# Counting the first 64 neighbours by scans along the rows, on the vector engine, in place of triangular matmuls on the tensor engine

## The chip, the cores and the metric

The kernel runs on one core of a Trainium2 chip. The core has a tensor engine (PE, whose weight loads stand as PEld), a vector engine (DVE), a scalar engine (ACT), GpSimd (POOL) and a sync engine (SP); each takes its instructions in order. The metric is the device time of one execution in microseconds (us), as the median of several.

## The reference

Four layers of a graph network over 2708 nodes with 512 features, joined by residuals and layer norms. The change lies in layer 0, and layer 1 uses what layer 0 makes of the adjacency matrix.

```python
# layer 0
Ab = A > 0
keep = Ab & (jnp.cumsum(Ab.astype(jnp.int32), axis=1) <= neibor_num)     # the first 64 neighbours of a row
cnt = keep.sum(axis=1, keepdims=True).astype(X.dtype)
nb_sum = keep.astype(X.dtype) @ X
nb_mean = nb_sum / jnp.maximum(cnt, 1.0)
xj = jax.nn.leaky_relu(nb_mean @ W_nb.T + b_nb)
xi = jax.nn.leaky_relu(X @ W_line.T + b_line)
return xi + jnp.where(cnt > 0, xj, jnp.zeros((), X.dtype))
# layer 1, in short
mask = (adj > 0).astype(x.dtype)
agg = mask @ x / jnp.maximum(mask.sum(axis=1, keepdims=True), 1.0)
```

Layers 2 and 3 are attention layers masked by `adj > 0`. Each layer's result is normed together with its input, `layernorm(x + layer(x))`.

## The kernel before

The 2708 rows lie in 22 tiles of 128 (the last has 20). `maskT` holds the whole adjacency matrix turned, in fp8, in SBUF: `maskT[:, j, :]` has neighbours 128j to 128j+127 on the partitions and all rows along the free dimension. Layers 0 and 1 use it as it is, and so do the attention layers, which want it as 0 and 1.

**First stage of layer 0.** The loop runs over the tiles t of rows. PE turns the tile of x (`transposed`, L120), multiplies it by the neighbour weight into PSUM tile `pm0` and by the line weight into `pm1` (`product`, L221: four fp32 matmuls each, which the profile shows as eight). `keep_y` splits `pm0` into a high part `yH` (ACT, L215) and the rest `yL` (DVE, L216). The second product gets its bias, its leaky ReLU and x, and goes to `r0_dram`. `load_mask` fetches a tile of the adjacency matrix (int32, cast to bf16 by the DMA, from POOL's queue), `count` makes it 0 and 1 and counts it on DVE (L240), then works out four columns of numbers from the count; `turn` transposes it on PE (L254) in three groups through the PSUM tiles `acc`, and ACT copies each group into `maskT` (L258). The masks have two buffers. `pe(...)` ties a PE instruction behind the one before it, so that the order is as written; where it isn't used, a scheduler orders the instructions by its own estimates. `tc.issue_after(i)` ties what stands in it behind instruction i on the same engine. At the start, `transpose_weight` turns the two weights (L132, copied by DVE at L133).

**The sums.** The rows are cut in six blocks (`cuts`): the last two tiles first, then five blocks of four tiles. For each block the loop runs over the 22 tiles j of neighbours; I call one pass a step. `kept` counts along j with a matmul by an upper triangle of ones (L311) into the running count `cum`, which another matmul by its complement (L401) brings to the end of tile j before the next; DVE compares the count with 64 and multiplies by the mask (L313), which gives `kT`, with two buffers:

```python
nc.tensor.matmul(cum[:, :w], upper, maskT[:, j, cols], start=(j == 0), stop=True, skip_group_check=True)
kT = st.tile([P, 512], F32R, name="kT", bufs=2)
nc.vector.scalar_tensor_tensor(kT[:, :w], cum[:, :w], KEEP, maskT[:, j, cols], op0=OP.is_le, op1=OP.mult)
```

Two matmuls for each row tile, by `yH` and by `yL`, add into its accumulator (L408: eight in a step of a full block, four in the first block's). At a block's end ACT scales the accumulators by `rkeep` (L418), and the block's `finish` (bias, leaky ReLU, `r0`, layer norm with a power on POOL at L113 and DVE's L114 behind it) runs among the next block's steps. Among them too run `weights1` (eight products of layer 1's weights) and `vectors` (24 pairs of DVE instructions, L388 and L389, for the later layers), which advance at every `next(later, None)`.

**Layer 1.** Its products loop over the tiles as in the first stage; its own sums (L450) read `maskT` through ACT casts (L447).

Of the kernel before, what the change touches and what calls it, by code (L numbers as in the profile page):

```python
# [30 lines left out]
def kernel(  # L31
# [44 lines left out]
    for c, value in ((iso, 0.0), (has, 0.0), (rdeg, 1.0), (rkeep, 1.0)):  # L76
        nc.vector.memset(c, value)
# [4 lines left out]

    maskT = big.tile([P, NT, NT * P], F8, name="maskT")
    nc.gpsimd.memset(maskT[:, NT - 1, :], 0.0)
    nc.gpsimd.memset(maskT[:, :, N:], 0.0)
# [39 lines left out]
    def transpose_weight(pool, psum, dst, src):  # L125

        for ki in range(KD):
            wr = pool.tile([P, D], F32, name="wr", bufs=4)
# [52 lines left out]
    def leaky(dst, u):  # L181
        nc.vector.scalar_tensor_tensor(dst, u, 0.01, u, op0=OP.mult, op1=OP.max)
# [7 lines left out]
    with ExitStack() as phase:  # L190
        yp = phase.enter_context(tc.tile_pool(name="y", bufs=1))

        upper = yp.tile([P, P], BF16, name="upper")
        make_upper_triangular(nc, upper)
        below = yp.tile([P, P], BF16, name="below")
        nc.vector.tensor_scalar(below, upper, -1.0, 1.0, op0=OP.mult, op1=OP.add)
# [16 lines left out]

        def keep_y(t, n, pm):
            nc.scalar.copy(yH[:n, t, :], pm[:n])  # L215
            return nc.vector.tensor_sub(yL[:n, t, :], pm[:n], yH[:n, t, :].bitcast(F32))  # L216
# [6 lines left out]

        def rows_of(src):
            return early(2, NT, lambda t: fetched(src, t, rows(t)))

        with ExitStack() as ph:
            st = ph.enter_context(tc.tile_pool(name="l0a", bufs=2))
            wnT, wlT = weight(), weight2

            def load_mask(t):
                n = rows(t)
                m = st.tile([P, N], BF16, name="m")
                nc.gpsimd.dma_start(m[:n], adj[t * P:t * P + n, :], max_dma_last_dim=N * 2)
                return m

            def count(t, m):
                n = rows(t)
                cnt = sm.tile([P, 1], F32, name="cnt")
                nc.vector.tensor_scalar(m[:n], m[:n], 0.0, None, op0=OP.is_gt, op1=OP.add, accum_out=cnt[:n])  # L240
                one = slice(t, t + 1)
                nc.vector.tensor_scalar(iso[:n, one], cnt[:n], 0.0, None, op0=OP.is_equal)
                nc.vector.tensor_scalar(has[:n, one], cnt[:n], 0.0, None, op0=OP.is_gt)
                nc.vector.tensor_scalar(rkeep[:n, one], cnt[:n], KEEP, 1.0, op0=OP.min, op1=OP.max)
# [993 lines left out]
```

## Time and profile before

| | |
|---|---|
| median of 6 runs | 3102.53 us (3101.47 to 3105.81) |
| the profiled execution | 3102.03 us, of it span 3100.2 us |
| busy share of the span | PE 97%, PEld 53%, DVE 64%, ACT 45%, POOL 7% |
| first stage of layer 0 | 0 to 216 us of the span |
| sums of layer 0 | 216 to 534 us |
| layer 1's products, its sums | 534 to 690 us, 690 to 940 us |
| attention layers and the end | from 940 us on |

A line of the profile's groups has the code line, the engine, the operation, out<-in with the tiles' names, partitions x elements and type, the count, then after the bar the busy time in us and the mean of one in ns, and after the second bar the idle time of the engine just ahead of these instructions with what ended it. A window's line has each engine's busy time with its count of instructions, then the granted clock of PE, the share of the DMA engines and what they moved.

### The profile page before, as it was taken

What the parts mean: (1) busy time and instruction counts of PE and PEld (TensorE: products, weight loads), DVE (VectorE), ACT (ScalarE), POOL (GpSimd) and SP (SyncE); (2) the same over time, 40 slices, a digit from 0 to 9 for tenths busy, and PEclk for the clock granted to TensorE, in tenths of its full rate; (3) what the DMA queues carried; (4) which work ended last, traced back from release to release, by engine and by line L of the source; (5) the groups of instructions that cost most, each with busy time, mean ns of one, the idle gap of its engine ahead of it and who ended that gap; (6) DMA issues with size and microseconds to landing.
All of it is one profiled execution on the core that took longest, in us unless ns stands there. A gap on an engine that the chain in (4) does not pass through costs nothing.

```text
span 3100.2 us, 37155 instructions
## 1 busy us (share of the span) xinstructions
PE 3000.7 (97%) x14888; PEld 1646.6 (53%) x14888; DVE 1988.8 (64%) x2562; ACT 1400.9 (45%) x1575; POOL 224.8 (7%) x352
## 2 busy tenths in 40 slices
PE   8999999999999999999998999999999999999998
PEld 4556666448888333333357333333367455555555
DVE  5662765212333899999987999999964534355342
ACT  2431000112224688888864888899873000000011
POOL 2220010101110000000012000000000000000001
PEclk9999999999999999999999999999999999999999
DMA  6651421322222000110024000010031000000000
GB/s 141 140 125 35 122 65 38 109 65 86 75 73 81 15 29 29 35 54 30 22 86 153 26 29 28 28 38 32 22 101 45 4 14 17 24 15 21 14 21 20
DMA packets 114287, 163.31 MB, mean 53 GB/s; under 512 B 39494, under 2 KB 62311, under 8 KB 114104
## 3 DMA queue, kind: packets, MB, share of 16 engines
q1 hardware_dynamic: 88152, 109.21, 11.6%
q0 software_dynamic: 16064, 47.95, 5.6%
q10 hardware_dynamic: 9888, 3.67, 0.5%
q8 instruction: 119, 1.95, 0.3%
q14 instruction: 64, 0.52, 0.1%
HBM read 130.92 MB, written 44.55 MB: 57 GB/s over the span
## 4 chain that ended last, share of the span: by engine, by line
PE 67%; issue 19%; DVE 10%; DMA 2%; ACT 2%; POOL 0%; SPq 0%; DVEq 0%; POOLq 0%; ACTq 0%
PE pn L869 13%; PE pm L221 10%; PE po L746 9%; PE acc L450 7%; DVE e L610 6%; PE pm L547 6%; PE acc L408 6%; PE pl L844 5%; PE pl L835 5%; PE pd L677 2%; PE ps_tr L120 1%; ACT c L618 1%; DMA rows<-o_dram 1%; PE acc L254 1%; PE pm L401 1%
## 5 line engine op out<-in xcount | busy, mean ns | idle before, releaser
L610 DVE SCALAR_TENSOR_TENSOR e<-v_bc,ucol,maskT 128x1300 f32<-128x1300 f32 (+3 forms) x836 | 1187.3, 1473 | 345.0 <-PE pn L869 317.8
L618 ACT ACTIVATE c<-e,bcol 128x1300 fp8e4<-128x1300 f32 (+1 forms) x704 | 994.0, 1423 | 112.0 <-DVE e L610 60.2
L746 PE MATMUL po<-e,R 128*64 128x512 f32 (+2 forms) x4224 | 947.0, 550 | 47.4 <-DVE e L610 47.2
L746 PEld LDWEIGHTS po<-e,R 128*64 128x64 f32 x4224 | 340.2, 136 | 601.3 <-issue 385.1
L869 PE MATMUL pn<-e,R 128*128 128x512 f32 (+1 forms) x1056 | 413.5, 542 | 0.2 <-ACT R L565 0.2
L869 PEld LDWEIGHTS pn<-e,R 128*128 128x128 f32 x1056 | 191.0, 190 | 199.6 <-issue 195.9
L547 PE MATMUL pm<-w,xT 128*128 128x264 f32 (+3 forms) x1056 | 247.7, 388 | 3.8 <-DVE R L561 3.0
L547 PEld LDWEIGHTS pm<-w,xT 128*128 128x128 f32 (+1 forms) x1056 | 193.0, 188 | 39.7 <-DVE R L561 3.6
L408 PE MATMUL acc<-yH,kT 128*128 128x512 f32 x484 | 214.0, 442 | 0.0
L837 ACT ACTIVATE w<-pl,b 128x256 f32<-128x256 f32 (+1 forms) x88 | 40.9, 465 | 372.9 <-PE pl L835 372.9
L450 PE MATMUL acc<-yH,mf 128*128 128x512 f32 x484 | 192.7, 398 | 0.0
L408 PE MATMUL acc<-yL,kT 128*128 128x512 f32 x484 | 192.1, 397 | 0.0
L450 PE MATMUL acc<-yL,mf 128*128 128x512 f32 x484 | 190.2, 393 | 0.0
L113 POOL TENSOR_TENSOR ln_rs<-ln_rs,half 128x1 f32<-128x1 f32 x88 | 51.5, 585 | 1710.7 <-DVE ln_rs L112 1710.6
L221 PE MATMUL pm<-w,xT 128*128 128x512 f32 (+1 forms) x384 | 173.1, 593 | 2.5 <-ACT xT L122 1.4
L221 PE MATMUL pm<-weight,xT 128*128 128x512 f32 (+1 forms) x352 | 162.3, 604 | 3.6 <-DVE weight L133 2.8
L313 DVE SCALAR_TENSOR_TENSOR kT<-pm,maskT 128x512 fp32r<-128x512 f32 (+1 forms) x132 | 84.7, 642 | 124.5 <-PE pm L311 123.9
L844 PE MATMUL pl<-lin,w 128*128 128x512 f32 (+1 forms) x352 | 157.4, 592 | 0.0
L835 PE MATMUL pl<-lin 128*128 128x256 f32 (+1 forms) x704 | 153.4, 371 | 3.7 <-DVE lin L768 3.7
L835 PEld LDWEIGHTS pl<-lin 128*128 128x128 f32 x704 | 129.1, 190 | 34.4 <-issue 15.8
L447 ACT CAST mf<-maskT 128x1024 fp32r<-128x1024 fp8e4 (+1 forms) x66 | 64.3, 976 | 164.1 <-PE acc L450 154.1
L215 ACT CAST yH<-pm 128x512 fp32r<-128x512 f32 (+1 forms) x44 | 25.7, 585 | 242.8 <-PE pm L221 242.8
(173 smaller groups left out, 2516.5 us busy)
## 6 DMA issues: line engine op xcount, KB each, us to landing
rows<-x_dram SPq DMA_DIRECT2D x63, 256.0 KB
m<-in_adj_dram POOLq DMA_DIRECT2D x21, 677.0 KB, 6.3
v_bc<-v_dram SPq DMA_DIRECT2D x16, 704.0 KB
x_dram<-u POOLq DMA_DIRECT2D x42, 256.0 KB, 2.3
rows<-o_dram SPq DMA_DIRECT2D x42, 256.0 KB
v_bc<-v_dram SPq DMA_DIRECT2D x16, 650.0 KB
o_dram<-o SPq DMA_DIRECT2D x32, 256.0 KB
rows<-in_x_dram SPq DMA_DIRECT2D x21, 256.0 KB
```

The lines of the kernel that those rows point to most:

```text
L221: order(nc.tensor.matmul(pm[:n], xT[:, k, :n], w[:, k, :], start=(k == 0), stop=(k == KD - 1)))
L313: nc.vector.scalar_tensor_tensor(kT[:, :w], cum[:, :w], KEEP, maskT[:, j, cols], op0=OP.is_le, op1=OP.mult)
L408: nc.tensor.matmul(pa[t], kT[:, (t - b[0]) * P:(t - b[0] + 1) * P], y[:, j, :], start=(j == 0 and y is yH), stop=(j == NT - 1 and y is yL))
L447: nc.scalar.copy(mf[:, :g1 - g0, :], maskT[:, g0:g1, t * P:(t + 1) * P])
L450: nc.tensor.matmul(pa, mf[:, j - g0, :], y[:, j, :], start=(j == 0 and y is yH), stop=(j == NT - 1 and y is yL))
L547: nc.tensor.matmul(pm[a][:n, :D // 2 + heads], xT[:, k, :n], w[:, k, a, :D // 2 + heads], start=(k == 0), stop=(k == KD - 1))
L610: nc.vector.scalar_tensor_tensor(e[:, :w], v[:, :w], ucol[:, j, h:h + 1], maskT[:, j, c0:c0 + w], op0=OP.max, op1=OP.mult)
L618: nc.scalar.activation(c[:, :w], e[:, :w], AF.Sigmoid, bias=bcol[:, j, h:h + 1], scale=STEP, saturate=False)
L746: pe(nc.tensor.matmul(po[i][HO * k:HO * k + HO, :c1 - c0], R2[:, j, h * HO:(h + 1) * HO], e[:, c0:c1], start=(j == 0), stop=(j == NT - 1)))
L835: nc.tensor.matmul(pl[:, :w], self.lin1[:, k, f * P:(f + 1) * P], h[:, k, :w], start=(k == 0), stop=(k == KD - 1))
L844: nc.tensor.matmul(pl[:n], gT[:, f, (t - t0) * P:(t - t0) * P + n], self.lin2[:, f, :], start=(f == 0), stop=(f == KF - 1))
L869: nc.tensor.matmul(pn[k][:, :w], R2[:, j, k * P:(k + 1) * P], e[:, :w], start=(j == 0), stop=(j == NT - 1))
```

## The change

The first 64 neighbours are found along each row, before the mask is turned. ACT makes the mask 0 and 1 by a steep sigmoid and counts it in passing (`count`). DVE runs a scan along the row that starts at -64.5, adds 1 at each neighbour and stops at 0.5, and multiplies the mask by it (`place`): a neighbour that is kept becomes negative, one that isn't becomes 0.5, the rest stays 0. The turned mask holds these numbers, and `kept` is a comparison with 0, without PE. In layer 1's products 22 DVE instructions make `maskT` 0 and 1 again. `place` works in two parts a mask in the first stage and in four parts in the sums.

The masks are taken in the order of the blocks (`turns`). 14 of the 22 pass through the first stage, with three buffers, spread over its tiles; every PE instruction there is bound by `pe`. The other eight go through `other_masks` among the steps of the sums, in two places of SBUF (`w` and `spare`), turned through `pm0` and `pm1`; `weights1` and `vectors` follow in the same chain, which now advances at every step, behind that step's `kept` (`issue_after`). The columns `has` and `rkeep` are worked out for each block at its end (`reciprocals`), `iso` and `rdeg` after the last mask. The raw weights of the start lie in `maskT` instead of buffers of their own, and `maskT`'s two memsets come after the first mask loads.

```diff
         def keep_y(t, n, pm):
-            nc.scalar.copy(yH[:n, t, :], pm[:n])
+            highs[t] = nc.scalar.copy(yH[:n, t, :], pm[:n])
             return nc.vector.tensor_sub(yL[:n, t, :], pm[:n], yH[:n, t, :].bitcast(F32))
...
+        HERE = NT - 8
+        cuts = [(b, min(b + 4, NT)) for b in range(0, NT, 4)]
+        cuts = cuts[-1:] + cuts[:-1]
+        turns = [t for b in cuts for t in range(*b)]
...
+        def count(i, m):
+            t, n = turns[i], rows(turns[i])
+            nc.scalar.activation(m[:n], m[:n], AF.Sigmoid, bias=gate[:n], scale=STEP, accum_out=cnts[:n, t:t + 1])
+
+        def place(i, m, places, part, of):
+
+            n = rows(turns[i])
+            c0, c1 = N * part // of, N * (part + 1) // of
+            nc.vector.tensor_tensor_scan(places[:n, :c1 - c0], m[:n, c0:c1], over[:n].to_broadcast([n, c1 - c0]),
+                                         places[:n, c0 - N * (part - 1) // of - 1:][:, :1] if part else -KEEP - 0.5,
+                                         OP.add, OP.min)
+            return nc.vector.tensor_mul(m[:n, c0:c1], m[:n, c0:c1], places[:n, :c1 - c0])
...
             for t in range(NT):
                 n = rows(t)
-                order = pe if t < 3 else as_it_comes
                 if t > 1:
-                    lows[t] = keep_y(t, n, product(xTs(t), n, wnT, 0, order))
+                    lows[t] = keep_y(t, n, product(xTs(t, order=pe), n, wnT, 0, pe))
                 xT = xTs(t)
                 if t + 1 < NT:
-                    xTs(t + 1)
-                for q in range(0 if t == 2 else t - 1, t) if t > 1 else ():
-                    turn(q, ms[q], order)
-                    if q + 2 < NT:
-                        ms[q + 2] = load_mask(q + 2)
-                pm = product(xT, n, wlT, 1, order)
+                    xTs(t + 1, order=pe)
+                while turned < counted - (t + 1 < NT):
+                    for _ in turn(turned, masks(turned), lambda: sums(BF16, (P, G, P)), pe):
+                        pass
+                    turned += 1
+                now = counted < min(HERE, -(-t * HERE // (NT - 4)))
+                if now:
+                    m, places = masks(counted), st.tile([P, N // 2], BF16, name="places", bufs=1)
+                    with tc.issue_after(highs[t].ins):
+                        count(counted, m)
+                    with tc.issue_after(lows[t].ins):
+                        place(counted, m, places, 0, 2)
+                pm = product(xT, n, wlT, 1, pe)
...
+                if now:
+                    with tc.issue_after(low.ins):
+                        place(counted, m, places, 1, 2)
+                    counted += 1
...
-            def kept(cum, b, j):
+            def kept(b, j):
                 cols, w = slice(b[0] * P, b[1] * P), (b[1] - b[0]) * P
-                nc.tensor.matmul(cum[:, :w], upper, maskT[:, j, cols], start=(j == 0), stop=True, skip_group_check=True)
                 kT = st.tile([P, 512], F32R, name="kT", bufs=2)
-                nc.vector.scalar_tensor_tensor(kT[:, :w], cum[:, :w], KEEP, maskT[:, j, cols],
-                                               op0=OP.is_le, op1=OP.mult)
-                return kT
+                made = nc.vector.tensor_scalar(kT[:, :w], maskT[:, j, cols], 0.0, None, op0=OP.is_lt)
+                return kT, made
...
+            def other_masks():
+
+                def room(i):
+                    r = (ahead.tile([P, 2 * KD * (D + 2 * H)], BF16, name="w", tag="w", bufs=1) if i % 2 else
+                         st.tile([P, 2 * KD * D], BF16, name="spare", tag="spare"))
+                    m = r[:, :N]
+                    load_mask(i, m)
+                    return m, r[:, N:N + N // 4 + 1]
+
+                got = {HERE: room(HERE)}
+                for i in range(HERE, NT):
+                    if i + 1 < NT:
+                        got[i + 1] = room(i + 1)
+                    m, places = got.pop(i)
+                    if i == HERE:
+                        for _ in range(5):
+                            yield
+                    count(i, m)
+                    yield
+                    yield
+                    for part in range(4):
+                        place(i, m, places, part, 4)
+                        yield
+                    psum = (ps_mm.tile([P, G, P], BF16, name=f"pm{k % 2}") for k in range(3))
+                    for _ in turn(i, m, lambda: next(psum)):
+                        yield
+                nc.vector.tensor_scalar(iso, cnts, 0.0, None, op0=OP.is_equal)
+                nc.vector.tensor_scalar(rdeg, cnts, 1.0, None, op0=OP.max)
+                nc.vector.reciprocal(rdeg, rdeg)
+
+            def reciprocals(ts_):
+                nc.vector.tensor_scalar(has[:, ts_], cnts[:, ts_], 0.0, None, op0=OP.is_gt)
+                one = rkeep[:, ts_]
+                nc.vector.tensor_scalar(one, cnts[:, ts_], KEEP, 1.0, op0=OP.min, op1=OP.max)
+                nc.vector.reciprocal(one, one)
...
-            todo, later = iter(()), chain(weights1(), vectors())
-            cum, kT = begin(cuts[0])
+            todo, both = iter(()), chain(other_masks(), weights1(), vectors())
+            kT, nxt_made = kept(cuts[0], 0)
...
                     next(todo, None)
-                    if i == 1 and j > 1 or i > 1 and j % 2 or i == 0 and j == 2:
-                        next(later, None)
+                    with tc.issue_after(nxt_made.ins):
+                        next(both, None)
+                with tc.issue_after(nxt_made.ins):
+                    reciprocals(slice(*b))
...
                 keep_y(t, n, product(xT, n, wnb[0], 0))
+                nc.vector.tensor_scalar(maskT[:, t, :], maskT[:, t, :], 0.0, None, op0=OP.not_equal, saturate=False)
                 if t + 1 < NT:
```

## The prediction

> **What bounds the kernel now.** I read the busy time by stage first, then the groups of layer 0, then the chain of waits there. Stretches of the span (columns: busy us of PE, PEld, DVE, ACT, POOL, then the granted clock, DMA share, GB/s):
>
> ```profile
> core 0: us, PE busy (x) PEld busy (x) DVE busy (x) ACT busy (x) POOL busy (x), PEclk, DMA share, GB/s
> 0.00:216.00 216.00, 203.14 (x957) 107.76 (x958) 124.45 (x217) 79.02 (x132) 60.92 (x76) 0.99 0.63 138
> 216.00:534.00 318.00, 314.00 (x1331) 215.04 (x1330) 177.36 (x318) 22.45 (x41) 24.69 (x38) 0.99 0.23 66
> 534.00:690.00 156.00, 155.28 (x424) 71.95 (x423) 41.35 (x69) 25.26 (x46) 15.90 (x29) 1.00 0.26 85
> ```
>
> The change touches these three: layer 0's first stage (0 to 216), its sums (216 to 534), layer 1's products (534 to 690). PE fills all three. Groups of the first two, with mean ns of one, then idle time before them:
>
> ```profile
> L408 PE MATMUL acc<-yH,kT 128*128 128x512 f32 x484 | 214.0, 442 | 0.0
> ...
> L313 DVE SCALAR_TENSOR_TENSOR kT<-pm,maskT 128x512 fp32r<-128x512 f32 x110 | 75.5, 686 | 112.7 <-PE pm L311 112.4
> L240 DVE TENSOR_SCALAR_CACHE_REDUCE m<-m 128x2708 bf16<-128x2708 bf16 x21 | 62.2, 2964 | 9.4 <-DMA m<-in_adj_dram 9.4
> L311 PE MATMUL pm<-maskT,upper 128*128 128x512 fp8e4 x110 | 41.7, 379 | 0.0
> L401 PE MATMUL pm<-maskT,below 128*128 128x512 fp8e4 x105 | 40.6, 387 | 2.1 <-DVE kT L313 2.1
> L254 PE MATMUL acc<-identb,m 128*128 128x128 bf16 x441 | 28.3, 219 | 0.5 <-DVE m L240 0.5
> ```
>
> Matmuls overlap, so these means aren't their cost: in the sums DVE waits for PE (112.7 us), PE for DVE 4.0 us in all. The cost is the pitch, which the chain of waits shows (start, us, what):
>
> ```profile
> 255.02 3.43 PE pm L221 x8
> ...
> 352.77 1.87 PE acc L408 x8
> 355.09 1.87 PE acc L408 x8
> 357.41 1.87 PE acc L408 x8
> ```
>
> One step of the sums is eight matmuls, 1.87 us (0.233 each), but steps start 2.32 us apart: the counting pair L401 and L311 costs 0.45. An x-row product (L221) takes 3.43.
>
> DVE's prices, from its groups:
>
> ```profile
> L388 DVE TENSOR_TENSOR spare<-spare 128x512 f32<-128x512 f32 x24 | 16.4, 683 | 2.9 <-DMA spare<-in_L_gnn_W_dram 1.9 <-DMA spare<-in_L_gnn_Wo_dram 0.8
> ...
> L765 DVE TENSOR_SCALAR spare<-rows 128x512 f32<-128x512 f32 x21 | 8.8, 424 | 21.8 <-DMA rows<-o_dram 21.7
> ```
>
> 512 elements cost 683 ns with two tensors and 424 with one tensor and constants; L240 (2708 in 2964) gives 1.04 ns an element and some 0.15 us fixed. In the timeline, back-to-back DVE instructions of 0.68 start 0.60 apart, so each costs its duration less 0.08.
>
> [...] Estimate: a new `kept` (512 columns) 0.42, a `not_equal` over 2816 columns 1.63.
> [...]
>
> ```profile
> 3.67 2.69 DVE L64 CAST identb<-ident 128x128 bf16<-128x128 f32 x1 [2.37 <-POOL ident masks.py:199]
> ...
> 3.60 2.07 POOL L85 MEMSET maskT<- 128x2376 fp8e4 x1
> ```
>
> A 128-column cast lasted 2.69 us under GpSimd's memset.
>
> **The change part by part.** The sums run from 217.8 to 533.5, 315.7 us; the six cuts take 27.6, 82.1, 52.3, 50.9, 51.3, 51.1 (starts of L408).
>
> *Counting pairs removed.* 110 steps x 0.45 + 22 narrow ones x (1.16-0.93) = **-54.6**. Left on PE: 968 x 0.233 = 225.5; layer 1's eight weight products, 8 x (3.43+0.44) = 31.0. The remaining 4.6 of the 315.7 are waits for `kT`, which also go.
>
> *Eight masks' transposes moved.* 22 start over 1.42 us in the first stage (113.36 to 114.78), so 8 x 1.42 = **-11.4** there and **+11.4** in the sums. PE's sums: 225.5+31.0+11.4 = 267.9.
>
> *DVE in the sums.* Each step has a `kept` of 0.34. Each mask part adds scan 1.49, product 0.43, and 0.1 for waiting on the scan: 2.37 with the `kept`, against 1.87 of PE. `kT` has two buffers, so DVE runs one step ahead at most, and its excess over a stretch, less one step, stops PE. I added up DVE's work between consecutive `kept`s, in the order in which the built kernel queues it, against PE's. Excesses: cut 0 3.4, cut 1 2.4, cut 2 5.2, cut 3 4.9, cut 4 none (PE has three weight products), cut 5 10.7. In cut 5's first nine steps stand the last vectors, four `finish`es and nine `kept`s, 29.9 us against 16.8; `not_equal`s follow. There PE gets layer 1's first products (7.3 us) early, covering 4.4. Together **+22.2**. The same addition on the kernel before gives 311.3 of the 315.7.
>
> *Waits added in the sums*, **+12**, each estimated. `u`'s scaling at a cut's end now waits for `reciprocals` behind a mask part; four accumulators wait for it: 2. The first mask's load starts when the first stage frees its buffer and shares the DMA with another's (6.3 us each alone, some 11 together, then 2.6 of count): its scan stands in front of step 9's `kept` and is 2.5 late. The 1 MB for layer 1's first weight product is asked for after the last mask left that buffer, three steps ahead (5.6 us), for some 8 us of transfer: 2.5. [...] L114 waited 6.2 us here before, and I add 5.
>
> *First stage.* Tiles start 8.83 us apart, of which the turn is 1.42. A tile with a mask gives DVE 2 x 2.94 + 2 x 0.88 + 3 x 0.61 = 9.5 us, one without 1.8. In runs of three or four mask tiles DVE falls 0.6 back per tile and then blocks the next but one product through L216: 4 over three runs. At the start the fourth copy of the second weight queues behind the first scan, which waits for yH, a table load and the count: pm1 starts at 28.8 instead of 27.0, **+1.8**. Mask DMAs issued before the memsets compete with weights: 1. With the turns: -11.4+4+1.8+1 = **-4.6**.
>
> *ACT.* A count is 2.55 us (L618: 1408 columns 1468 ns, 1300 1378), a turn's casts 2.65; with 1.2 of copies 6.4 of 8.83: hidden. In the sums ACT was busy 22 of 318; 8 x 5.2 more hide.
>
> *SP and POOL.* Eight mask loads cross into the sums, where the DMA share was 0.23; they pass r0 and weight loads, and the waits are those above.
>
> *Layer 1.* The other 13 `not_equal`s add 20 us to DVE's 41 of 156. PE waits for DVE only once a whole product behind (3.43), more than two of them: 0.
>
> **Sum.** Sums 267.9+22.2+12 = 302.1 (-13.6), first stage -4.6: **-18.2**. The profiled execution is 3102.03 (span 3100.2 and 1.8 around it), 0.5 under the median 3102.53: 3083.8 against it, **3084** against the median. A measurement of this kernel can tell some 0.2% (6 us) from no change.
>
> **Unknown costs.** Scan: 0.86 (full rate) to 2.2; I take 1.57. At full rate the sums lose 12 more and the first stage 4; at 2.2 the sums gain 20. Product: 0.51 or 0.86; at 0.86 +10 in the sums, +8 in the first stage. `kept`: 0.42 or 0.69. The 12 of waits: 0 to 22.
>
> **The rivals.**
> 1. *DVE keeps up* (0.17): its excess disappears in slack that I don't see. The sums are 268 to 275, the first stage -11: 3050. For it: in the trace DVE's 43 us in 350 to 400 held PE up by 1.5. Against: 2.37 against 1.87 stands in four steps of each mask.
> 2. [...] (0.11): +18, 3102, no change. No trace row excludes it.
> 3. [...] (0.12), slower. Place: `kept` and `not_equal` on DVE. Price: 0.69 and 3.1. The same addition gives the sums 29 more, mainly in cut 5 (nine `not_equal`s at 3.0 beside 1.87): 3113. It decides from a `kept` of about 0.60. [...]
> 4. *The masks come late* (0.08): [...] ACT's count and DVE's queue wait: 22 x some 1.5 = +33, 3117.
>
> **How the numbers follow.** My case has 0.52. Faster takes it nearly whole (0.50), rival 1 (0.17), a third of rival 2 (0.04) and a little of 3 (0.02): 0.73. Same: rest of mine 0.02, 0.04 of rival 2, 0.03 of the others: 0.09. Slower: 0.18. The range runs from rival 1 (3050) to short of rival 3's value (3110).
>
> **What would show it.** In the profile after: L408's steps 1.87 apart where no mask or `finish` is, longer in cut 2, 3 and 5, PE idle there put down to DVE's `kT`; the scan at 1.57 and 3.0, the product at 0.51, `kept` at 0.42. A scan near 0.86 or a `kept` near 0.69 breaks a price; sums under 285 or over 315 us break the addition; a first stage over 218 breaks its slack.

## The result, and the profile after

The kernel after takes 3094.88 us (median of 17 runs, 3091.37 to 3101.13), the kernel before beside it 3102.28 (37 runs): ratio 0.9977, 95% interval 0.9971 to 0.9984, or 7.4 us less. The forecast was 18.2 us less. The profiled execution after took 3093.61 us, of it span 3091.8.

The windows of the kernel after, as the prediction shows them of the kernel before (columns: busy us of PE, PEld, DVE, ACT, POOL, then the granted clock, the DMA share and GB/s):

```profile
0.00:216.00 216.00, 185.26 (x737) 94.36 (x738) 161.06 (x132) 92.70 (x125) 90.25 (x64) 0.97 0.45 105
216.00:534.00 318.00, 293.25 (x1292) 208.71 (x1291) 218.82 (x410) 68.51 (x90) 44.49 (x49) 0.99 0.36 90
534.00:690.00 156.00, 156.00 (x433) 72.84 (x432) 64.03 (x90) 26.16 (x47) 27.34 (x30) 1.00 0.25 84
```

PE fills the first stage no longer: 185 of 216 us for 203 before. POOL went from 61 to 90 us there, although the change gives it fewer loads there and no new instruction: something holds its instructions up. DVE's groups in the first stage, then POOL's addition of x to `u` in the kernel after and, as L292, in the kernel before:

```profile
L245 DVE TENSOR_TENSOR_SCAN places<-m,places,over 128x1354 bf16<-128x1354 bf16 x13 | 39.4, 3031 | 0.0
L245 DVE TENSOR_TENSOR_SCAN places<-m,over 128x1354 bf16<-128x1354 bf16 x13 | 38.7, 2977 | 10.8 <-ACT m L239 10.4
L248 DVE TENSOR_TENSOR m<-m,places 128x1354 bf16<-128x1354 bf16 x26 | 32.1, 1234 | 0.6
```

```profile
L311 POOL TENSOR_TENSOR u<-u,rows 128x512 f32<-128x512 f32 x21 | 63.7, 3035 | 123.3 <-DVE u L179 123.3
L292 POOL TENSOR_TENSOR u<-u,rows 128x512 f32<-128x512 f32 (+1 forms) x22 | 27.9, 1268 | 117.8 <-DVE u L182 117.8
```

The scans have the forecast price (3.0). The products (L248) average 1234 ns where the forecast assumed 860 (its 0.88 is that, with 0.1 of waiting and less 0.08), and POOL's addition 3035 for 1268 before. The timeline of one mask tile puts the two side by side (start, us, what), DVE and then POOL:

```profile
40.01 3.03 DVE L245 TENSOR_TENSOR_SCAN places<-m,places,over 128x1354 bf16<-128x1354 bf16 x1
43.08 1.75 DVE L248 TENSOR_TENSOR m<-m,places 128x1354 bf16<-128x1354 bf16 x1
44.74 0.68 DVE L216 TENSOR_TENSOR yL<-pm,yH 128x512 fp32r<-128x512 f32 x1
```

```profile
40.19 3.91 POOL L311 TENSOR_TENSOR u<-u,rows 128x512 f32<-128x512 f32 x1 [2.33 <-DVE u L179]
```

The second scan starts 0.2 us ahead of the addition; the addition ends 1.06 us after the scan, and the product then ends 0.73 after the addition. In all 14 mask tiles the addition starts 0.2 us behind a scan and lasts 3.91 to 3.93 us; in the seven full tiles without a mask it lasts 1.26 or 1.27. `yL`, which frees PE's `pm0`, stands behind the product. PE's waits in the first stage (in total, times, longest):

```profile
PE pm L221 <- DVE yL L216: 16.3, 9, 2.4
...
PE pm L221 <- DVE weight L130: 5.2, 1, 5.2
```

And PE after three such waits, with a window on each of the first two products:

```profile
66.19 5.29 PE L221 MATMUL pm<-w,xT 128*128 128x512 f32 x8 [2.45 <-DVE yL L216]
104.45 3.67 PE L221 MATMUL pm<-w,xT 128*128 128x512 f32 x8 [2.45 <-DVE yL L216]
143.50 5.37 PE L221 MATMUL pm<-w,xT 128*128 128x512 f32 x8 [2.44 <-DVE yL L216]
```

```profile
66.10:69.40 3.30, 3.21 (x4) 1.51 (x5) 3.05 (x2) 0.22 (x2) 0.22 (x1) 0.50 0.86 207
104.40:108.20 3.80, 3.75 (x11) 1.81 (x12) 3.15 (x2) 3.15 (x7) 0.19 (x1) 1.00 0.86 184
```

After the first idle of 2.45 us the granted clock was 0.50 for a while and the product took 5.29 us; after the second, as long, it took the usual 3.67. Of five waits of 2.2 to 2.5 us in this stage two were followed by such a slow product (5.29 and 5.37), some 3.4 us together.

Later stages hold a surprise. Layer 1's sums, whose instructions the change leaves alone, took 225.7 us before and take 219.3. The chain in a stretch of 30 us, the kernel before and then after:

```profile
799.91 30.10 PE acc L450 x129
```

```profile
799.97 30.15 PE acc L495 x133
```

30.10/129 is 0.2333 us a matmul, 30.15/133 is 0.2267.

So the time by stages, from profiles. "Start" runs from the second product with the first weight to the third, "tiles" from there to the first matmul of the sums. (In the profiles of this document that second product starts between 16.5 and 25.5 us, with the arrival of the first weights; that is left out here.)

| us | start | tiles | layer 0's sums | layer 1's products | layer 1's sums |
|---|---|---|---|---|---|
| before | 19.9 | 181.1 | 315.3 | 162.2 | 225.7 |
| after | 21.3 | 188.4 | 311.2 | 153.5 | 219.3 |
| forecast change | first stage: -4.6 | | -13.6 | 0 | 0 |

The first two of layer 1's products now start inside the sums, as forecast. At the forecast's 7.3 us for the pair the sums proper fell by 11.4 and the products by 1.4. The first stage is 8.7 longer. From layer 1's sums come 6.4 that no step of the forecast had. (Each row of these tables is a single profile. The programs e5, e8, e11 and e15 below have the kernel after's first stage, instruction for instruction; over the five the tiles took 188.4 to 191.9 us, with two to four slow products. A difference of 3 us in that column says little.)

### The profile page after: what moved, and what is told of

The parts are those of the page before. It is cut to its first block, busy times and chain, and to the rows that moved or that the text cites. A ratio compares the mean times of both kernels' runs of the same rounds, so it can differ in the third digit from the quotient of the medians.

```text
span 3091.8 us, 36738 instructions
## 1 busy us (share of the span) xinstructions
PE 2955.0 (96%) x14630; PEld 1629.6 (53%) x14630; DVE 2088.9 (68%) x2589; ACT 1462.1 (47%) x1621; POOL 286.0 (9%) x350
## 3 DMA queue, kind: packets, MB, share of 16 engines
q1 hardware_dynamic: 88152, 109.21, 11.6%
q10 hardware_dynamic: 9888, 3.67, 0.5%
## 4 chain that ended last, share of the span: by engine, by line
PE 61%; issue 20%; DVE 13%; ACT 3%; DMA 2%; POOL 1%; SPq 0%; DVEq 0%; POOLq 0%; ACTq 0%
PE pn L914 13%; PE po L791 9%; PE pm L221 8%; PE acc L495 7%; PE pm L592 7%; DVE e L655 6%; PE pl L889 5%; PE pl L880 5%; PE acc L450 4%; PE pd L722 2%; PE ps_tr L117 1%; DVE places L245 1%; ACT c L663 1%; DVE w L245 1%; DVE spare L245 1%
## 5 line engine op out<-in xcount | busy, mean ns | idle before, releaser
L450 PE MATMUL acc<-yH,kT 128*128 128x512 f32 x484 | 200.3, 415 | 18.7 <-DVE kT L327 12.8
L592 PEld LDWEIGHTS pm<-w,xT 128*128 128x128 f32 (+1 forms) x1056 | 192.2, 187 | 38.9 <-DVE R L606 4.0
L221 PE MATMUL pm<-w,xT 128*128 128x512 f32 (+1 forms) x384 | 177.0, 604 | 17.0 <-DVE yL L216 16.3
L495 PE MATMUL acc<-yH,mf 128*128 128x512 f32 x484 | 188.4, 389 | 0.0
L221 PE MATMUL pm<-weight,xT 128*128 128x512 f32 (+1 forms) x352 | 161.8, 602 | 6.5 <-DVE weight L130 5.2
L722 PE MATMUL pd<-c,parts_c 128*12 128x384 fp8e4 (+2 forms) x2816 | 130.9, 307 | 0.0
L221 PEld LDWEIGHTS pm<-w,xT 128*128 128x128 f32 (+1 forms) x384 | 71.6, 189 | 112.4 <-issue 103.0
```

What stands on the lines that cost most here:

```text
L221: order(nc.tensor.matmul(pm[:n], xT[:, k, :n], w[:, k, :], start=(k == 0), stop=(k == KD - 1)))
L450: nc.tensor.matmul(pa[t], kT[:, (t - b[0]) * P:(t - b[0] + 1) * P], y[:, j, :], start=(j == 0 and y is yH), stop=(j == NT - 1 and y is yL))
L495: nc.tensor.matmul(pa, mf[:, j - g0, :], y[:, j, :], start=(j == 0 and y is yH), stop=(j == NT - 1 and y is yL))
L592: nc.tensor.matmul(pm[a][:n, :D // 2 + heads], xT[:, k, :n], w[:, k, a, :D // 2 + heads], start=(k == 0), stop=(k == KD - 1))
L722: pe(nc.tensor.matmul(p[32 * g:32 * g + 12, :c1 - c0], parts_c[:, j, h, :], c[:, c0:c1], start=(j == 0 and h == hs[0]), stop=(j == NT - 1 ...
```

## The experiments

**The first stage.** The theory after these lines: GpSimd's addition, started behind a scan, takes 3.91 us for 1.27, and the product, the stores and the loads behind it come late. The rival: three or four mask tiles in a row are too much for DVE, whatever GpSimd does. e1 is the kernel before once more. e2 leaves out the addition of x (its r0 lacks x), e3 the counting itself (the rows of these masks keep all neighbours); in e4 the masks are spread over more tiles; in e7 the addition is DVE's.

```diff
# e1_before_again: the kernel before, unchanged
# e2_no_add
-                nc.gpsimd.tensor_add(u[:n], u[:n], xs(t))
+                xs(t)
# e3_no_place_first: both place(...) of the first stage left out
# e4_even
-                now = counted < min(HERE, -(-t * HERE // (NT - 4)))
+                now = counted < min(HERE, -(-t * HERE // (NT - 2)))
# e7_add_on_dve
-                nc.gpsimd.tensor_add(u[:n], u[:n], xs(t))
+                low = nc.vector.tensor_add(u[:n], u[:n], xs(t))
```

> The kernel before, once more, beside the next three on one chip. Disputed: in the kernel after the matmuls of layer 0's sums follow each other every 0.2265 us instead of 0.233, and layer 1's sums, whose instructions the change does not touch, are 6.4 us shorter (219.3 for 225.7). If that is the program's doing (where its tiles lie, or the counting left out), this run shows 0.233 and 225.7 again and its neighbours 0.2265. If it is the chip or the execution, this run shows the same figures as its neighbours.

> The kernel after without GpSimd's addition of the rows to u in the first stage (r0 then lacks x; everything else stays). Theory: the addition and the second scan meet, the addition takes 3.9 us for 1.3, the second product of a mask waits for it (1.75 us for 0.86), and the r0 store and the next mask's load go out late. Then the second products fall to 0.86, the stalls of the first stage go, the first stage falls from 226.8 by 10 to 18 us, and the ratio to before is 0.992 to 0.995. Rival (the vector engine has too much to do in a run of three or four mask tiles, 9.5 us against TensorE's 8.8, whatever GpSimd does): the first stage falls by 4 us at most, ratio 0.996 to 0.998.

> The kernel after without the scans and products of the 14 masks of the first stage (their rows then keep all neighbours); loads, ScalarE's counts and transposes stay. It gives the floor of the first stage. Theory (the vector engine's part costs it all): the kernel before's 217.8 less the 11.4 us of eight masks' transposes, 206 to 208, so that scans and products cost 19 to 21 us in the kernel after. Rival (the order of counts, transposes and loads costs it, not the scans): 215 or more. The rest of the kernel stays within 2 us of the kernel after.

> The kernel after with its 14 masks spread over tiles 1 to 19 instead of 1 to 17 (NT - 2 for NT - 4 in the line that sets them), so that runs are two or three long instead of three or four, all instructions kept. If runs are what costs: the stalls halve, the first stage is 6 to 10 us shorter, ratio 0.994 to 0.996. If the meeting of addition and scan costs the same in every mask tile whatever its neighbours: 0 to 4 us, ratio 0.996 to 0.998. A loss is possible at the end, where the last masks are turned with less work beside them.

> The kernel after with the addition of the rows to u moved from GpSimd to the vector engine, behind the leaky step and ahead of the second scan. Theory (meeting of addition and scan): the second products fall from 1.6 to 0.86 us, the vector engine gains 0.69 per tile in return, and the r0 stores and mask loads leave on time; a mask tile has about the same work as in the kernel after (10.2 for 10.4), so the first stage gains only what the late loads cost, 2 to 6 us, ratio 0.996 to 0.997. Rival (only the amount of the vector engine's work counts): 0 to 2 us either way, ratio 0.997 to 0.998.

| us | start | tiles | whole, ratio to before |
|---|---|---|---|
| e1, before again | 19.9 | 181.4 | 3103.97 (one run) |
| e2, no addition | 22.3 | 176.3 | 3084.76, 0.9940 (0.9926 to 0.9953) |
| e3, no scans | 15.5 | 166.6 | 3065.11, 0.9883 (0.9867 to 0.9898) |
| e4, spread | 22.6 | 188.6 | 3095.08, 0.9978 (0.9969 to 0.9986) |
| e7, addition on DVE | 22.7 | 182.7 | 3086.23, 0.9950 (0.9937 to 0.9964) |

The products of e2, and PE's wait:

```profile
L248 DVE TENSOR_TENSOR m<-m,places 128x1354 bf16<-128x1354 bf16 (+1 forms) x28 | 24.1, 860 | 0.6
```

```profile
PE pm L221 <- DVE yL L216: 8.5, 9, 1.6
```

860 ns is what the forecast assumed: the rest of 1234 was the addition. The waits halve, and the tiles fall by 12.1 us, to under the kernel before: 7.8 from these waits, some 3.4 because no product in e2's tiles ran at the low clock (the first weight's matmuls, L221, average 596 ns between 20 and 206 us, for 621 in the kernel after). So the theory holds for about 12 of the 21.8 us that the tiles stand above their floor, which is e3's time (188.4 less 166.6). One part of it does not count: the loads do come late, but DVE doesn't feel it. ACT's counts waited for them in the kernel after, and not in e2 (second line), while e2's first scans waited for ACT 9.9 us (third line), nearly the 10.4 shown above:

```profile
ACT m L239 <- DMA m<-in_adj_dram: 14.6, 4, 4.8
L239 ACT ACTIVATE m<-m,gate 128x2708 bf16<-128x2708 bf16 (+1 forms) x14 | 35.7, 2553 | 0.0
L245 DVE TENSOR_TENSOR_SCAN places<-m,over 128x1354 bf16<-128x1354 bf16 (+1 forms) x14 | 41.6, 2974 | 10.3 <-ACT m L239 9.9
```

The other 9.7 stay without any addition: in e2 the mask tiles of a run of four start 8.8, 10.3, 9.6 and 9.6 us apart, the last two about DVE's work in a tile (9.5 in the prediction), for 8.8 with no scans (e3). So the rival holds for that part. e4 shows that shorter runs alone bring nothing while addition and scan still meet: tiles 11.6 us long come in runs of two as in runs of three. Moving the addition to DVE (e7) costs DVE 0.69 us a tile (L311, mean 691) and still gains 5.7 in the tiles; its mask tiles within a run are 9.3 to 10.3 long.

e3's first stage is below the 206 to 208 expected, and it gives the floor of the start as well: 15.5 for 21.3. There the fourth copy of the second weight waits for no mask; in the kernel after PE's 5.2 us on L130 are this. In the kernel before the old count stood ahead of the same copy, and PE paid with a wait and a slow product:

```profile
27.00 5.40 PE L221 MATMUL pm<-weight,xT 128*128 128x512 f32 x8 [2.83 <-DVE weight L133]
```

e1 reads like the first profile of before, layer 1's sums 225.7 again, while its neighbours on the same chip have 219.3: the pace belongs to the program, not to the chip.

**The pace of layer 1's sums.** The instructions are the same, so what is left are values, places in SBUF and what went before. In the built programs' allocation `yH` and `yL` (the moving operand of both layers' sums) start 32 bytes off a multiple of 64 in the kernel before and on one in the kernel after, since smaller tiles now lie ahead of them. The runs below only leave gaps between tiles.

```diff
# e5_after_pad and e6_before_pad (both gaps), e9_before_shift (the first gap only)
+        yp.tile([P, 8], F32, name="pad0")
         weight2 = yp.tile([P, KD, D], F32, name="weight2")
         ...
         yL = yp.tile([P, NT, D], F32R, name="yL")
+        yp.tile([P, 8], F32, name="pad1")
# e13_before_gap448, e14_before_gap64, e18_before_gap192, e15_after_gap64: only
+        yp.tile([P, 112], F32, name="pad1")    # 448 bytes; 16: 64 bytes; 48: 192 bytes
```

> The kernel after with 32 bytes per partition left free in front of weight2, yH and yL and 32 more behind them: yH and yL, the moving operands of both layers' sums, then start 32 bytes off a multiple of 64, as in the kernel before; all later tiles move by 64 and keep their place to a multiple of 64. No instruction is changed. Theory (the place of yH and yL sets the pace of the matmuls, 0.2267 or 0.2334 us): layer 1's sums 219.3 to 225.7, layer 0's sums 311 to 317, the whole 12 to 13 us longer, 3107, ratio 1.001 to 1.003. Rival (another difference between the two programs sets it, the place of the weights kT and mf or the counting): 219.3 stays, ratio 0.998.

> The kernel before with the same two gaps of 32 bytes: its yH and yL then start at a multiple of 64. No instruction is changed. Theory: both layers' sums fall by 6 to 6.5 us each (315.3 to 309, 225.7 to 219.3), the whole by 12 to 13, 3090, ratio 0.9958, so that these 64 bytes alone bring more than the whole change. Rival: 225.7 stays and the ratio is 1.000.

> The kernel before with one gap of 32 bytes per partition in front of weight2: yH and yL and everything allocated behind them, kT and mf among it, then start at a multiple of 64, as in the kernel after. No instruction is changed. With yH and yL alone moved the pace stayed at 0.2343 us, with yH and yL off and the weights on a multiple at 0.2333. Theory now (the matmul runs at 0.2267 only when moving operand and weights both lie at a multiple of 64 bytes): layer 1's sums 225.7 to 219.3, layer 0's 315.3 to about 310, the whole 11 to 13 us shorter, ratio 0.996 to 0.9965. Rival (the pace comes from something else in the kernel after): 225.7 and ratio 1.000.

> The kernel before with a gap of 448 bytes per partition behind yL: yH and yL stay where they are (32 bytes off a multiple of 64), kT and mf move, so that the distance from yH to mf is the kernel after's to a multiple of 512 (256; before 320). No instruction is changed. In the runs so far the pace went with this distance and not with the place of either: distance 64 past a multiple of 256 (before, and before with everything moved by 32) 231 and 236 ns in turn, 32 past (after with its gaps) 232 and 235, 96 past (before with its gaps) 231 to 238, none (after) 227. Theory (the distance of weights and moving operand to a multiple of 256 bytes sets the pace): 227 ns in both, layer 1's sums 225.7 to 219.3, layer 0's 315.3 to 309 or 310, ratio 0.996 to 0.9965. Rival (something else in the kernel after, its values or its order): 225.7 and ratio 1.000.

> The kernel before with a gap of 64 bytes behind yL: distance 128 past a multiple of 256. If the multiple that counts is 64 or 128, the pace is 227 ns and layer 1's sums 219.3; if it is 256, the pace is 231 to 238 ns and the sums stay at 225 to 227.

> The kernel after with a gap of 64 bytes behind yL: the distance from yH to kT and mf becomes that of the kernel before to a multiple of 512 (320), all else stays. Theory (distance): matmuls 231 and 236 ns in turn as in the kernel before, layer 1's sums 219.3 to 225.7, layer 0's sums 2 to 6 us longer, ratio 1.000 to 1.002 for 0.998. Rival (something else in the kernel after): 227 ns, 219.3, ratio 0.998.

> The kernel before with a gap of 192 bytes behind yL: the distance from yH to kT and mf is then a multiple of 512 (the kernel after and the gap of 448 have 256 past one; the gap of 64 has 384 past one and was slow). If a multiple of 256 is what counts, the matmuls run at 227 ns, layer 1's sums take 219.3 and the ratio is 0.9975; if it is 256 past a multiple of 512, 231 ns or more, 225 or more and 1.000.

In the table, the first figures are the bytes by which `yH` and `mf` (the weights of layer 1's sums) start past a multiple of 64. The distance is the start of `mf` less that of `yH`, as what is left over a multiple of 512; that of `kT`, the weights of layer 0's sums, is the same in each program. (From one step to the next it changes by a multiple of 512.) The time from one matmul to the next is that of layer 1's sums.

| kernel | `yH`, `mf` past 64 | distance past 512 | ns from one matmul to the next | layer 1's sums | layer 0's sums | whole, ratio |
|---|---|---|---|---|---|---|
| before | 32, 32 | 320 | 231, 236 | 225.7 | 315.3 | 1 |
| e9, before shifted | 0, 0 | 320 | 231, 236 | 225.7 | 317.4 | 3102.17, 0.9999 (0.9990 to 1.0007) |
| e15, after + 64 | 0, 0 | 320 | 231, 236 | 225.7 | 313.4 | 3101.34, 0.9999 (0.9991 to 1.0008) |
| e6, before padded | 0, 32 | 352 | 230 to 238 | 226.6 | 315.6 | 3101.11, 1.0002 (0.9994 to 1.0010) |
| e5, after padded | 32, 0 | 288 | 232, 235 | 225.7 | 312.9 | 3101.40, 0.9996 (0.9988 to 1.0004) |
| e14, before + 64 | 32, 32 | 384 | 228 to 241 | 224.8 | 314.6 | 3099.23, 0.9993 (0.9985 to 1.0002) |
| after | 0, 0 | 256 | 227 | 219.3 | 311.2 | 3094.88, 0.9977 (0.9971 to 0.9984) |
| e13, before + 448 | 32, 32 | 256 | 227 | 219.3 | 313.7 | 3093.49, 0.9975 (0.9966 to 0.9984) |
| e18, before + 192 | 32, 32 | 0 | 227 | 219.3 | 314.8 | 3093.12, 0.9969 (0.9959 to 0.9980) |

e5 and e6 seemed to say that both operands must lie on a multiple of 64; e9, which has both, refuted it. What the fast kernels share is the distance: a multiple of 256. 320 gives the same two numbers in turn in three programs, whatever lies at which address. Neither place decides alone: before, e13, e14 and e18 have `yH` at the same address, and two are fast; e5 and e15 have `mf` at the same address, and their numbers differ. The chain of e13 and e15, in the stretch shown above:

```profile
799.89 30.15 PE acc L451 x133
```

```profile
799.84 30.33 PE acc L496 x130
```

e13 reads like the kernel after and e15 like the one before, each in the other's program: e13 is the kernel before with nothing changed but 448 empty bytes, and is as fast as the kernel after; e15 is the kernel after with 64 empty bytes, and is as fast as the kernel before. Within the interval of e15 the whole measured gain is this distance. Why the hardware does this no run shows. Layer 0's sums gain far less: 2.2 us in the kernel after (e15 against it), 1.6 and 0.5 in the kernel before (e13, e18), where e13 was expected to gain some 6; before and e9, with the same distance, lie 2.1 apart. In the traces of e13 and e18 many of its matmuls still follow each other at 231 to 236 ns; in the kernel after those of undisturbed steps do so at 227, those near a wait at up to 236.

**The sums of layer 0.** The eight masks' scans were priced at 22.2 us of stalls, the waits at 12.

```diff
# e8_no_place_sums
                     for part in range(4):
-                        place(i, m, places, part, 4)
                         yield
# e11_sixths
-                    count(i, m)
+                        count(i, m)    # now under the test for the first mask
...
-                    for part in range(4):
-                        place(i, m, places, part, 4)
+                    for part in range(6):
+                        place(i, m, places, part, 6)
                         yield
+                    if i + 1 < NT:
+                        count(i + 1, got[i + 1][0])
```

> The kernel after without the scans and products of the eight masks among layer 0's sums (their rows keep all neighbours); their loads, counts and transposes stay. Theory (the vector engine's walk as predicted, 22.2 us of stalls less what the pace of the matmuls has changed): the sums fall from 311.2 by 15 to 22 us. Rival (what holds the sums above TensorE's own work are the ends of the cuts, layer 1's weights and the reciprocals): they fall by 8 us at most.

> The kernel after with the scans and products of the eight masks among the sums cut in six parts instead of four, one a step (about 1.95 us with its kT for a step of TensorE of 1.81, instead of 2.5), and a mask's count ahead of the turn of the one before instead of behind it. Theory (four steps in a row that are each 0.7 us too long for the vector engine are what stalls kT): the waits for kT fall by half or more and the sums from 311 by 5 to 10 us, ratio 0.9945 to 0.996. Rival (only the sum of the vector engine's work counts, which is slightly more): 2 us either way.

e8, whose rows of these masks keep all neighbours: 291.6 us of sums for 311.2, ratio 0.9921 (0.9905 to 0.9936). The scans cost 19.6, within the 15 to 22 expected. PE's waits for `kT` in the kernel after, then the two longest of e8:

```profile
PE acc L450 <- DVE kT L327: 12.8, 16, 1.8
```

```profile
PE acc L449 <- ACT u L461: 6.4, 4, 3.4
PE acc L449 <- DVE kT L327: 3.7, 5, 1.2
```

Some 3.3 of the 19.6 are again low clock, an estimate: half the clock over these 6.6 us of the kernel after; in e8's sums the granted clock is 1.00 over the whole stage:

```profile
308.50:315.10 6.60, 5.51 (x13) 4.24 (x14) 3.91 (x8) 3.05 (x6) 0.00 (x0) 0.50 0.12 32
```

What remains in e8 are mainly the ends of the cuts, where the scaling of `u` waits for the reciprocals. e11: 301.1 us of sums, 3083.05, ratio 0.9938 (0.9925 to 0.9952). Its waits for `kT` are 8.3, down by a third, not by half as expected, but the sums fell by 10.1, the upper end of the 5 to 10 expected. A part is now 1143 ns of scan and 392 of product (451 columns), so a step's DVE work, with its `kept`, is close to PE's. The edit also moves the count, so how much of the 10.1 is due to which isn't separated.

**Towards a faster version.**

```diff
# e10_quarters (core): three quarters a tile from tile 2 on, ahead of u, which is tied behind them
+                    with tc.issue_after(lows[t].ins):
+                        for q in range(placed, min(placed + 3, 4 * HERE)):
...
+                            last = place(i, *held[i], q % 4, 4)
...
+                if t > 0 and 4 * counted < min(placed + 3, 4 * HERE):
+                    count(counted, masks(counted))     # a tile ahead, behind the casts
# e12_all: e10 and e11, and reciprocals of the 14 first blocks ahead of the sums
# e16_combined: e7 and e11, and
+                now = counted < min(HERE, -(-(t - 1) * HERE // (NT - 4)))
# e17_halves_spread (core), on e16: piece() counts a mask at its first half and places one half;
# u is tied behind it, and a mask is turned behind the second product of its tile
+                aim = min(2 * HERE, -(-max(t - 1, 0) * 2 * HERE // 19))
+                last = piece(t, lows[t]) if done < aim else lows[t]
                 pm = product(xT, n, wlT, 1, pe)
...
+                if done < aim:
+                    piece(t, low)
+                while turned < full:
```

> The kernel after with the 14 scans of the first stage cut in quarters instead of halves and laid out evenly: three quarters in every tile from 2 to 20, between yL and the addition of the bias, so that GpSimd's addition falls behind them; the count of a mask runs a tile ahead, and loads are asked for when a buffer has been turned. Theory (runs, the wait for the count and the meeting of addition and scan cost the first stage 22 us over its floor of 166.6 from tile 2 on): the vector engine has 8.0 to 8.4 us a tile for TensorE's 8.3, the products of tile 2 on come at 7.4 to 8.9 us, and tile 2 to the first sum takes 168 to 175 instead of 188; with the fourth weight copy no longer behind a scan the start is 4 us shorter; ratio 0.990 to 0.993. Rival (the vector engine is too full in any layout): 182 or more, ratio 0.996.

> Both (quarters in the first stage, sixths among the sums), and the reciprocals of the 14 blocks counted in the first stage made ahead of the sums instead of at the end of each cut. If the three are independent: the sum of the gains of the two kernels run beside it, and 1 to 3 us more from the ends of the cuts, ratio 0.985 to 0.989. If the sums' stalls come back elsewhere (the vector engine is late at the first cut): less than the larger of the two plus 3 us.

> The kernel after with three edits that the runs point to: the addition of the rows on the vector engine (its run alone gave 0.9950), the sums' masks in sixths (0.9938 alone; after itself 0.9977), and the first stage's masks begun a tile later, at tile 2, so that no scan stands ahead of the fourth copy of the second weight. If the gains add: 0.9950 + 0.9938 - 0.9977 = 0.9911, less 4 to 6 us at the start of the first stage, 0.989 to 0.990 (3068 to 3072). If the sums take back what the first stage gives, or the later start lengthens a run of seven masks: 0.991 to 0.993.

> The combined kernel before it (addition on the vector engine, sums in sixths, first mask at tile 2) with the 28 half scans of the first stage shared out over tiles 2 to 20, one or two a tile instead of two or none, and the transposes of a mask behind the second product of their tile instead of ahead of it, one tile after its last half. Theory (a tile with two halves, 10.3 us of the vector engine, is what TensorE waits for; the total, 8.2 us a tile, is not): tile 2 to the first sum falls from 187 to 170 to 178, ratio 0.987 to 0.989 for 0.9919. Rival (three buffers and the loads of 8 us set the pace of the masks, as in the kernel of quarters): 187 or more, ratio 0.992 or worse.

| us | start | tiles | layer 0's sums | whole, ratio to before |
|---|---|---|---|---|
| e10 | 15.6 | 206.8 | 314.5 | 3113.77, 1.0036 (1.0022 to 1.0049) |
| e12 | 15.5 | 206.7 | 304.1 | 3105.34, 1.0010 (1.0002 to 1.0019) |
| e16 | 17.2 | 186.9 | 300.9 | 3075.11, 0.9919 (0.9905 to 0.9933) |
| e17 | 17.2 | 175.1 | 306.2 | 3068.85, 0.9887 (0.9870 to 0.9903) |

e10 lies far from both expectations (168 to 175 us of tiles, or 182 and more with a ratio of 0.996); ACT's groups show where it stood:

```profile
L239 ACT ACTIVATE m<-m,gate 128x2708 bf16<-128x2708 bf16 x10 | 25.5, 2552 | 74.0 <-DMA m<-in_adj_dram 74.0
```

ACT stood 74 us in front of counts whose masks hadn't landed, and the `yH` copies stood behind. A mask's load is queued on POOL behind an addition and an r0 store that wait for DVE, then takes 8.0 us to land: with three buffers this reads as a loop: load, count, scans, addition, load. No run took this loop apart, and e10 says nothing of DVE's total. Additions took 1263 ns again there, since no scan starts just ahead of them. Here the addition comes first and the scan behind it is the longer one, 2.26 us for 1.63:

```profile
107.23 1.26 POOL L321 TENSOR_TENSOR u<-u,rows 128x512 f32<-128x512 f32 x1 [10.55 <-DVE u L179]
107.66 2.26 DVE L245 TENSOR_TENSOR_SCAN places<-m,places,over 128x677 bf16<-128x677 bf16 x1
```

e12, expected at 0.985 to 0.989, has e10's first stage. Making reciprocals early brought nothing that shows in its sums: 304.1 for e11's 301.1, and e10's are 3.3 longer than the kernel after's too.

e16 gains less than the sum of its parts: the later start saves 4 us in "start", and the tiles give it back, 186.9 for e7's 182.7, in a first run of four masks. e17 spreads the halves without counting ahead. Its waits in the first stage:

```profile
PE pm L221 <- DVE u L316: 3.2, 6, 1.9
PE pm L221 <- DVE yL L216: 1.1, 1, 1.1
```

The 16.3 us on `yL` are 1.1, and the tiles took 175.1, inside the 170 to 178 expected, with more DVE work than the kernel after has. So with the addition out of the scans' way it was the distribution over tiles, not DVE's total, that held PE up (the turns' later place, and another place for the loads, came with it and weren't tried apart). The sums give 5.3 us back, of which 4.7 is one wait of their first accumulator for the last casts (PE acc L464 on L261). e17 beats both kernels: 33.6 us under the kernel before beside it.

## Why the prediction was wrong

**Prices: right.** Scan 1.61 and 3.0 us (forecast 1.57, 3.0), product of 677 columns 508 ns (0.51), `kept` 417 ns (0.42), `not_equal` 1616 ns (1.63):

```profile
L245 DVE TENSOR_TENSOR_SCAN w<-w,over 128x677 bf16<-128x677 bf16 x16 | 25.8, 1611 | 0.1
L248 DVE TENSOR_TENSOR w<-w 128x677 bf16<-128x677 bf16 x16 | 8.1, 508 | 0.1
L327 DVE TENSOR_SCALAR kT<-maskT 128x512 fp32r<-128x512 fp8e4 x110 | 45.8, 417 | 63.2 <-PE acc L450 63.1
L474 DVE TENSOR_SCALAR maskT<-maskT 128x2816 fp8e4<-128x2816 fp8e4 x10 | 16.2, 1616 | 0.0
```

`kept` and `not_equal` were estimates from L765 (424 ns for 512 columns). The prices of scan and product were my assumptions: no line of before shows either. From their two sizes here a further column costs the scan 2.0 ns ((2977 - 1611)/677) and the product 0.52 ((860 - 508)/677, 860 from e2), where L240 showed 1.04. Rival 2 (0.86 for the product of 677 columns) and rival 3 (0.69 and 3.1) are out; so is rival 1, with 303.9 us of sums proper for its 268 to 275.

**The step that failed** is in "First stage": "In runs of three or four mask tiles DVE falls 0.6 back per tile ...: 4". Measured on e3's floor, scans cost the tiles 21.8 us, of which GpSimd's addition makes 12.1 (e2). The working had priced that addition at nothing and the product behind it at 0.86. The lines that should have warned stand in the prediction: a DVE cast of 128 columns that lasted 2.69 us, where GpSimd's memset of 2.07 had started 0.07 ahead of it (at L388's pace, 683 ns for 512 columns, I estimate under 0.3 for such a cast). The working drew nothing from them for the scans. The runs show the same: an addition behind a scan takes 3.91 us for 1.27, and in e10 a scan behind an addition 2.26 for 1.63. In these three the second to start was the long one; `yL`, started beside a running addition in five tiles of the kernel after, took 0.65 to 0.67, no longer than elsewhere (0.68). What makes the one wait for the other no run shows. Rival 4 had the loads late, and they were (ACT's counts waited 14.6 us for them), but what cost time was the addition and the product behind it. The remaining 9.7 (for 4) are DVE's excess in runs, where `yL` stands behind the second product.

The start came out about as forecast: +1.4 us for 1.8 and 1 (the table load that it names lasts 1.28 us, ahead of the first count on ACT; the 1 for the mask loads was an estimate, and no run shows it apart). In the tiles, what the change takes away was worth 14.5 (e3 against before) for 11.4: in e3 a tile with a turn takes 8.83 us and one without 7.31, so eight turns make some 12, and no run splits the rest. Together: 1.4 - 14.5 + 21.8 = +8.7 for a forecast -4.6. The forecast had no term for the low clock behind a wait, which is some 3.4 of the 21.8.

**The sums: right in total, by two errors.** Forecast 302.1; measured 311.2 less the 7.3 of layer 1's products, 303.9. Scans among the sums cost 19.6 for 22.2 (e8), so the walk along DVE's queue held. With the forecast's 267.9 of PE's own work, which is at the old pace, the waits would be 16. At the new pace PE's own would be 968 x 0.2267 + 31.0 + 11.4 = 261.8, so 22.5 are left where 12 were put (12.8 of them are PE's waits in e8, the largest for `u`; the rest no run splits), and the faster matmuls hid part of it. At the old distance (e15) the sums are 313.4.

**"Layer 1: 0"** was right for what the change does to its instructions, and 6.4 us wrong for its sums. Nothing in the profile of before could show it; that matmuls of the same shape ran 231 and 236 ns in turn there was to be read, but not that 227 was to be had.

**The sum.** First stage +8.7, sums and layer 1's products -12.8, layer 1's sums -6.4, the rest +2.1 make the profiled -8.4. At equal distance the change is worth 0.9999 (0.9991 to 1.0008): what it gains in the sums it loses in the first stage. That the time fell at all, as forecast, was luck: it fell by an effect that the forecast didn't contain.

## What to carry to other kernels

Work moved to one engine can lengthen what runs beside it on another: here a GpSimd addition went from 1.27 to 3.91 us behind a DVE scan, and DVE's product behind that from 0.86 to 1.75. List the GpSimd instructions that new DVE instructions will meet, and price the pair, not the parts. Spread such work in pieces no longer than the slack of a tile or step, and keep it from standing in front of the instruction that frees a single-buffered accumulator. When a stage that wasn't edited changes its time, compare the pace of its instructions and the addresses of its operands before crediting the edit.

## What was not expected of the hardware

- fp32r matmuls (128x128 by 512) follow each other at 0.2267 us where the distance in SBUF from moving operand to weights is a multiple of 256 bytes, and at 0.2324 to 0.2343 where it is 32, 64, 96 or 128 past one: layer 1's sums in nine layouts of two programs. The matmul records of the fp32 products (L221, eight a product) follow each other at 0.43 us in both programs.
- Waits of 2.2 to 2.5 us were followed by a granted clock of 0.50 for some 3 us in two of five cases in one trace (PE's next product 5.29 and 5.37 us for 3.67); in e17 one of 1.9 us was (5.40). What decides it no run shows. So a wait can cost PE its own length and some 1.7 us more.
